# Two attention-and-mixture layers on one core: the second layer norm of sequence 0 placed beside the last block of the first attention, and the second layer's weights loaded into the first layer's tiles

## The chip, the cores and the metric

The kernel runs as one program on one core of a Trainium2 chip. The metric is the device time of that core in microseconds (us), the median of three executions. One more execution was recorded by the hardware profiler; all stretches of time below come from it.

## The reference, cut to what matters

The input is x with 2 sequences of 2048 tokens and 256 features, all float32. Two layers follow each other:

```python
xn = layernorm(x)
s  = attention0(xn)                 # 16 heads of 16 features, every token sees every token
g  = silu(ffn0(xn))                 # mixture of 16 low-rank branches, cumulative sums over the tokens
x  = x + s * g
xn = layernorm(x)
s  = attention1(xn)                 # 16 heads, a token sees only tokens at most 64 away
g  = silu(ffn1(xn))                 # dense base plus 8 low-rank experts with softmax gates
x  = x + s * g
```

`layernorm` takes mean and variance over the 256 features of each token, with eps 1e-5 and no scale or shift.

## The kernel before

**Layout.** Features lie on the 128 partitions (two chunks `c`), tokens along the free axis, in blocks of `TB` = 512 tokens (four blocks `n` for each sequence `b`). `x`, `xn` and `gt` stay in SBUF for both sequences. The program is traced once by a tile framework, which places waits and also decides each engine's order, from the order of the calls and its own estimates; what is wrapped in `keep_in_program_order` holds its place.

**Stages in order of time.** Weights and the first layer norm; the first ffn; the first attention (`attention(A0, ..., False, False)`, called at L840); the second layer norm with the gates (`layer_norms`, L95, called at L937, for eight blocks: both sequences); the second ffn (`experts`, L899); the second attention.

**First attention.** An item is one sequence, one group `g` of four heads and one block `n` of 512 queries: 32 items, 16 steps each, one step per 128 keys (`U` = 16). A step of the *second pass* of an item computes, for each of the four heads, the scores of 128 keys against the 512 queries on the PE (`sk`, L599, four concurrent row tiles of 32 rows), their exponentials on ScalarE (`e`, L615), and the weighted sum of the values on the PE (`acc`, L662, in `weigh`), which ScalarE copies out of PSUM (`av` or `more`, L669 and L672) and GpSimd adds up (L673). The *first pass* of an item, which finds the maximum of each query's scores, runs 19 steps ahead (`sq`, L599; its reduction on VectorE, L611). So in each step one item's first pass lies beside another item's second pass. In the last 19 steps (`LEAD` = 3 and the 16 of the last item) there is no first pass left. I number them s0-3 to s0+15, where s0 is the first step of the last item.

**PSUM in the first attention.** There are 8 banks of 128x512 float32. `pmax` (tag `sq`) has two tiles of two banks each; `pexp` (called `pm`, tag `m`) has four of one bank. While both passes run, the four `sk` and the `acc` of a step take five tiles from the four banks of `pm` in turn, and the two pairs of `sq` take `pmax`. In the last 19 steps the branch `not apart and j >= 2` (L559) puts two of the four `sk` into the idle `pmax` (`sk2`), so that a step takes only three tiles from `pm`.

**Order in a step.** `scores` issues the step's `sk` (and `sq`); then `weigh` issues the `acc` of the step before (`DEL` = 1); then come the calls that `at(step, f)` has put behind that step: the sums of an item are scattered by DMA, inverted and multiplied (`compact` to `divide`), and for the last group of heads two products with the output weights (`project`, L756: tile `pr`, then `upd` on VectorE, then an addition on GpSimd).

**Second layer norm.** For a block, `there` turns x on the PE so that tokens lie on the partitions (`xt`, L104, eight 128x128 transposes), takes mean and variance on VectorE (L108, L110), and forms two factors (`Sqrt` on ScalarE, L113, reciprocal and product on VectorE). `back` applies them on ScalarE (`xc`, L121), turns the result back (`xb`, L127, eight transposes) and copies it to `xn` (L129, one copy on each of ScalarE and VectorE). Between blocks the gates' logits of the block before are computed (`gates`, `tokens`); `normalized` is the softmax over experts and `turned` spreads the gates over partitions by way of DRAM.

**Weights.** `load_attn` loads the four matrices and four biases of an attention. The second layer's are loaded after the first attention is through (L845, on the SP queue), and the four tensors of its ffn on the ScalarE queue (L851 to L854).

## Time and profile before

| what | value |
|---|---|
| median of three executions | 2620.93 us (2620.79 to 2621.52) |
| the profiled execution | 2619.84 us, of which the span of the program 2618.1 us |
| granted TensorE clock, mean over the span | 0.991 |
| busy share of the span: PE, VectorE, ScalarE, GpSimd | 98%, 64%, 63%, 34% |

In the rows below PE is TensorE's matmuls and PEld its weight loads, DVE is VectorE, ACT ScalarE, POOL GpSimd, SP the queue of most DMAs. A row of the timeline gives the start, the time until its last instruction ends, the engine, the source line, what is written from what, and the count; in brackets stands the idle time before it and what ended that. The ends of matmuls are modelled, and consecutive instructions of one engine overlap, so the distance between starts is the better measure of a rate.

### The profile page before, as it was taken

What the parts mean: (1) busy time and instruction counts of PE and PEld (TensorE: products, weight loads), DVE (VectorE), ACT (ScalarE), POOL (GpSimd) and SP (SyncE); (2) the same over time, 40 slices, a digit from 0 to 9 for tenths busy, and PEclk for the clock granted to TensorE, in tenths of its full rate; (3) what the DMA queues carried; (4) which work ended last, traced back from release to release, by engine and by line L of the source; (5) the groups of instructions that cost most, each with busy time, mean ns of one, the idle gap of its engine ahead of it and who ended that gap; (6) DMA issues with size and microseconds to landing.
All of it is one profiled execution on the core that took longest, in us unless ns stands there. A gap on an engine that the chain in (4) does not pass through costs nothing.

```text
span 2618.1 us, 49275 instructions
## 1 busy us (share of the span) xinstructions
PE 2570.3 (98%) x19060; PEld 1099.6 (42%) x19060; DVE 1671.5 (64%) x2753; ACT 1641.1 (63%) x3200; POOL 894.9 (34%) x845
## 2 busy tenths in 40 slices
PE   8999999999999999999999999999999978999999
PEld 5444444543333333333333333333333324558776
DVE  4133332167888888888777888888888523228884
ACT  5300000228888888888778888888888854236655
POOL 0000000203444444444444444444444430206666
PEclk9999999999999999999999999999999989989999
DMA  4031110410001010010010010010000012411120
GB/s 150 3 88 45 53 45 32 99 64 4 8 12 19 8 24 9 6 25 8 6 25 8 6 25 8 6 27 6 8 8 6 10 30 35 96 67 39 46 58 35
DMA packets 58857, 82.08 MB, mean 31 GB/s; under 512 B 24160, under 2 KB 29152, under 8 KB 57040
## 3 DMA queue, kind: packets, MB, share of 16 engines
q1 hardware_dynamic: 56576, 77.36, 12.3%
q8 instruction: 150, 2.46, 0.4%
q10 hardware_dynamic: 2048, 1.58, 0.2%
q14 instruction: 83, 0.68, 0.1%
HBM read 52.22 MB, written 21.95 MB: 28 GB/s over the span
## 4 chain that ended last, share of the span: by engine, by line
PE 97%; DVE 1%; ACT 1%; DMA 0%; issue 0%; POOL 0%; SPq 0%; POOLq 0%; ACTq 0%; DVEq 0%
PE sk L599 25%; PE acc L662 22%; PE sq L599 19%; PE pp L446 4%; PE py L377 4%; PE po L357 4%; PE px L373 4%; PE ph L263 2%; PE pr L761 2%; PE pp L459 2%; PE psf L199 1%; PE po L909 1%; PE tr L687 1%; PE xb L127 1%; PE po L389 1%; PE xt L104 1%
## 5 line engine op out<-in xcount | busy, mean ns | idle before, releaser
L611 DVE TENSOR_REDUCE part<-sq 128x2 f32<-128x1024 f32 x1024 | 1206.7, 1220 | 304.2 <-PE sq L599 303.7
L615 ACT ACTIVATE e<-sk 128x512 f32<-128x512 f32 x2048 | 1062.7, 615 | 214.9 <-PE sq L599 192.2
L599 PE MATMUL sk<-q,k 32*128 32x512 f32 (+2 forms) x5632 | 1149.7, 533 | 0.6 <-ACT e L615 0.4
L599 PE MATMUL sq<-k,q 32*128 32x512 f32 (+2 forms) x5120 | 1140.8, 572 | 3.2 <-DVE part L611 1.7
L673 POOL TENSOR_TENSOR av<-av,more 128x512 f32<-128x512 f32 x480 | 607.7, 1266 | 961.2 <-ACT more L672 961.1
L599 PEld LDWEIGHTS sk<-q,k 32*128 32x128 f32 x5632 | 532.3, 184 | 581.1 <-ACT e L615 490.9
L662 PE MATMUL acc<-e,v 128*32 128x512 f32 x4096 | 550.6, 605 | 0.0
L599 PEld LDWEIGHTS sq<-k,q 32*128 32x128 f32 x5120 | 412.5, 184 | 28.0 <-DVE part L611 14.0
L672 ACT COPY more<-acc 128x512 f32<-128x512 f32 x480 | 287.8, 600 | 3.8 <-PE acc L662 1.7
L662 PEld LDWEIGHTS acc<-e,v 128*32 128x32 f32 x4096 | 82.4, 108 | 391.5 <-ACT e L615 387.0
L393 ACT ACTIVATE gt<-po 128x512 f32<-128x512 f32 x16 | 9.5, 596 | 324.6 <-PE po L389 324.6
L606 DVE CUSTOM_DVE_ANT_0 seen<-sq,mask 128x256 f32<-128x256 f32 (+1 forms) x512 | 177.4, 411 | 41.5 <-PE sq L599 32.8
L399 POOL TENSOR_TENSOR x<-x,up 128x512 f32<-128x512 f32 x16 | 20.2, 1264 | 416.4 <-DVE up L396 416.4
L620 POOL TENSOR_SCALAR_AFFINE_SELECT xn<-xn 128x512 f32<-128x512 f32 x172 | 103.1, 635 | 119.3 <-ACT xn L615 117.4
L381 DVE TENSOR_TENSOR xs<-we,px 128x512 f32<-128x512 f32 x64 | 43.8, 685 | 135.4 <-PE px L373 135.4
L373 PE MATMUL px<-xn,FV 128*128 128x512 f32 x256 | 121.2, 595 | 0.0
L377 PE MATMUL py<-cum,FW 128*128 128x512 f32 x256 | 120.5, 593 | 0.6 <-DVE cum L346 0.6
L615 ACT ACTIVATE xn<-sk 128x512 f32<-128x512 f32 x172 | 90.1, 601 | 48.2 <-PE sk L599 12.9
L357 PE MATMUL po<-pr,UO 128*128 128x512 f32 x256 | 119.0, 592 | 0.0
L383 DVE TENSOR_TENSOR pr<-xs,py 128x512 f32<-128x512 f32 x64 | 44.0, 687 | 62.4 <-PE py L377 62.2
L766 DVE TENSOR_TENSOR upd<-gt,pr 128x512 f32<-128x512 f32 x32 | 22.0, 687 | 86.0 <-PE pr L761 79.5
L357 PEld LDWEIGHTS po<-pr,UO 128*128 128x128 f32 x256 | 48.6, 190 | 61.2 <-issue 60.7
(169 smaller groups left out, 1683.2 us busy)
## 6 DMA issues: line engine op xcount, KB each, us to landing
we<-wd SPq DMA_DIRECT2D x128, 128.0 KB
qd<-sb SPq DMA_DIRECT2D x48, 256.0 KB
k<-qd SPq DMA_DIRECT2D x40, 128.0 KB
q<-qd SPq DMA_DIRECT2D x40, 128.0 KB
x<-in_x SPq DMA_DIRECT2D x8, 512.0 KB
q<-row SPq DMA_DIRECT2D x256, 2.0 KB
xn<-av SPq DMA_DIRECT2D x128, 32.0 KB
recb<-rd SPq DMA_DIRECT2D x128, 32.0 KB
```

What stands on the lines that cost most here:

```text
L357: nc.tensor.matmul(po[oc], UO[:, ch, bass.ts(oc, P)], pr, start=(ch == 0), stop=False)
L373: nc.tensor.matmul(px, FV[:, c, bass.ts(ch, P)], xn[b][:, c, cols], start=(c == 0), stop=(c == NC - 1))
L377: nc.tensor.matmul(py, FW[:, c, bass.ts(ch, P)], cum[:, c, :], start=(c == 0), stop=(c == NC - 1))
L446: nc.tensor.matmul(ps, w[:, c, bass.ts(hf, P)], xn[b][:, c, bass.ts(n, TB)], start=(c == 0), stop=(c == NC - 1))
L599: nc.tensor.matmul(o, lhs, rhs, start=True, stop=True)
L606: nc.vector.tensor_tensor_reduce(seen[:, lo:hi], sq[:, d, t * 2 * P + lo : t * 2 * P + hi], mask[:, lo:hi], 1.0, LOWEST, ALU.add, ALU.max, ...
L611: nc.vector.tensor_reduce(pt[:, pair[0] : pair[1] + 1, t, kb], sq, AX.X, ALU.max)
L615: nc.scalar.activation(e, t, AF.Exp, scale=scale)
L620: nc.gpsimd.affine_select(out=e[:, :, c, :], in_=e[:, :, c, :], compare_op=ALU.is_ge, fill=0.0, base=0, pattern=[[0, 4], [sign, P]], chann ...
L662: nc.tensor.matmul(acc[hp[j], o : o + hi - lo], vs[b][:, kt, vcols(g, j)], es[j][:, lo:hi], start=(r == 0), stop=(r == len(parts) - 1), sk ...
L672: nc.scalar.copy(more, acc)
L673: nc.gpsimd.tensor_tensor(avs[i], avs[i], more, ALU.add)
```

## The change

- `layer_norms` is split: `there`, `factors` and `back` can be used apart, and the second call handles only sequence 1 (four blocks).
- The four blocks of sequence 0 get their second layer norm within the last 16 steps of the first attention, two blocks at a time: `norm_there` behind s0 and s0+1 (and s0+8, s0+9), `norm_factors` for both blocks behind s0+2 (s0+10), `norm_back` behind s0+3 and s0+5 (s0+11, s0+13). `xt` takes the tiles of `pmax`, `xb` those of `pm`, `xc` those of the exponentials. VectorE, not ScalarE, applies the factors and makes both copies to `xn`.
- In the last 19 steps all four `sk` of a step come from `pm` (`tail`).
- The sums `av` and `more` of the last item are copied out of PSUM by VectorE instead of ScalarE.
- After the attention the gates and the softmax of sequence 0 come first, then the layer norms of sequence 1 with `turned` of sequence 0 and the gates of sequence 1 between them.
- The attention weights of both layers share tiles (`wat`). The second layer's q and k and the two low-rank factors of its ffn (in the tile of `wv`) are loaded at step 0 of the first attention, its o after it, its v after `experts`. Its biases, `gateT` and `baseT` are loaded with the first layer's weights.

```diff
-                        if not apart and j >= 2:
+                        if not apart and not tail and j >= 2:
...
+                copy = nc.vector.tensor_copy if not local and i == len(items) - 1 else nc.scalar.copy
...
                 elif u == 0:
-                    nc.scalar.copy(avs[i], acc)
+                    copy(avs[i], acc)
                 else:
                     more = op.tile([P, TB], F32, name="more", tag="more", bufs=2)
-                    nc.scalar.copy(more, acc)
+                    copy(more, acc)
...
+                def norm_there(n):
+                    if n % 2 == 0:
+                        norms["mv"] = op.tile([P, 2 * QT, 2], F32, name="mv", tag="mv")
+                    xt = norms[n] = pmax.tile([P, QT, D], F32, name="xt", tag="sq")
+                    st = op.tile([P, QT, 6], F32, name="st", tag="st")
+                    there(0, n, xt, norms["mv"][:, n % 2 * QT : (n % 2 + 1) * QT, :], st, pin)
+                def norm_factors():
+                    norms["f"] = op.tile([P, 2, 2 * QT], F32, name="nf", tag="nf")
+                    factors(norms["f"], norms["mv"], pin)
+                def norm_back(n):
+                    xt, f, xc = norms.pop(n), norms["f"], []
+                    for t in range(QT):
+                        if t % 2 == 0:
+                            xc.append(ep.tile([P, 2, D], F32, name="xc", tag="e"))
+                        r = n % 2 * QT + t
+                        nc.vector.tensor_scalar(
+                            xc[-1][:, t % 2, :], xt[:, t, :], f[:, 0, r : r + 1], f[:, 1, r : r + 1], ALU.mult, ALU.add
+                        )
+                    for c in range(NC):
+                        xb = pm.tile([P, TB], F32, name="xb", tag="m")
+                        for t in range(QT):
+                            nc.tensor.transpose(xb[:, bass.ts(t, P)], xc[t // 2][:, t % 2, bass.ts(c, P)], ident)
+                        nc.vector.tensor_copy(xn[0][:, c, bass.ts(n, TB)], xb)
+                for r in range(NB // 2):
+                    s0 = total - U + r * (U // 2)
+                    at(s0, norm_there, 2 * r)
+                    at(s0 + 1, norm_there, 2 * r + 1)
+                    at(s0 + 2, norm_factors)
+                    at(s0 + 3, norm_back, 2 * r)
+                    at(s0 + 5, norm_back, 2 * r + 1)
...
+    def second_weights():
+        pin = tc.keep_in_program_order
+        A1.update(q=weight(1, "q", pin), k=weight(1, "k", pin))
+        t = wat.tile([P, NC, D], F32, name="lUV", tag="wv")
...
-    attention(A0, 1.0 / float(np.sqrt(D)), False, False)
-    layer0.close()
+    attention(A0, 1.0 / float(np.sqrt(D)), False, False, second_weights)
...
-            blocks = [(b, n) for b in range(B) for n in range(NB)]
             held = {}
+            for n in range(NB + 1):
+                if n < NB:
+                    held[n] = gates(pg1, 0, n)
+                if n:
+                    tokens(pg1, *held.pop(n - 1))
+            normalized(0)
             def between(r):
+                if r == 1:
+                    turned(pg1, 0)
                 if r - 1 in held:
                     tokens(pg1, *held.pop(r - 1))
-                if 1 <= r <= len(blocks):
-                    held[r] = gates(pg1, *blocks[r - 1])
-                if r == NB + 1:
-                    normalized(0)
-                if r == NB + 3:
-                    turned(pg1, 0)
-            layer_norms(blocks, tb, pn1, between)
+                if r:
+                    held[r] = gates(pg1, 1, r - 1)
+            layer_norms([(1, n) for n in range(NB)], tb, pn1, between)
```

In the built program GpSimd's order is as before, and every other engine's order differs only from s0 to the end of the second layer norm, apart from where the weights' DMAs stand on their queues.

More of the change, by code (lines that the diff above doesn't have):

```diff
@@ L71, in rows, with weight, biases @@
         return ap.rearrange("(c p) m -> p c m", p=P)
-    def load_attn(pool, l, eng):
-        return dict(
-            q=load(pool, f"wq{l}", [P, NC, D], rows(a[f"wq{l}"]), eng),
-            k=load(pool, f"wk{l}", [P, NC, D], rows(a[f"wk{l}"]), eng),
-            v=load(pool, f"wv{l}", [P, NC, D], rows(a[f"wv{l}"]), eng),
-            o=load(pool, f"wo{l}", [P, NC, D], rows(a[f"wo{l}"]), eng),
-            bq=load(pool, f"bq{l}", [P, NC], a[f"bq{l}"], eng),
-            bk=load(pool, f"bk{l}", [P, NC], a[f"bk{l}"], eng),
-            bo=load(pool, f"bo{l}", [P, NC], a[f"bo{l}"], eng),
-            bv=load(pool, f"bv{l}", [P, NC], a[f"bv{l}"], eng),
-        )
+    wat = ctx.enter_context(tc.tile_pool(name="wat", bufs=1))
+    def weight(l, kind, issue=lambda i: i):
+        t = wat.tile([P, NC, D], F32, name=f"w{kind}{l}", tag=f"w{kind}")
+        issue(nc.sync.dma_start(out=t, in_=rows(a[f"w{kind}{l}"])))
+        return t
+    def biases(l):
+        return {b: load(wat, f"{b}{l}", [P, NC], a[f"{b}{l}"], nc.sync) for b in ("bq", "bk", "bo", "bv")}
     def whole_bias(A, ps):
@@ L93, in whole_bias, with there, factors, go @@
         nc.vector.tensor_tensor(A["bo"], A["bo"], ps[:, :NC], ALU.add)
+    QT = TB // P
+    def there(b, n, xt, mv, st, first=lambda i: i):
+        for t in range(QT):
+            for c in range(NC):
+                i = nc.tensor.transpose(xt[:, t, bass.ts(c, P)], x[b][:, c, bass.ds(n * TB + t * P, P)], ident)
+                if t + c == 0:
+                    first(i)
+        for t in range(QT):
+            nc.vector.bn_stats(st[:, t, :], xt[:, t, :])
+        for t in range(QT):
+            nc.vector.bn_aggr(mv[:, t, :], st[:, t, :])
+    def factors(f, mv, issue=lambda i: i):
+        issue(nc.scalar.activation(f[:, 0, :], mv[:, :, 1], AF.Sqrt, bias=eps_t))
+        nc.vector.reciprocal(f[:, 0, :], f[:, 0, :])
+        nc.vector.scalar_tensor_tensor(f[:, 1, :], mv[:, :, 0], -1.0, f[:, 0, :], ALU.mult, ALU.mult)
     def layer_norms(blocks, tmp, ps, between=lambda r: None):
-        QT = TB // P
-        def there(b, n):
+        def go(b, n):
             xt = ps.tile([P, QT, D], F32, name="xt", tag="xt")
-            for t in range(QT):
-                for c in range(NC):
-                    nc.tensor.transpose(xt[:, t, bass.ts(c, P)], x[b][:, c, bass.ds(n * TB + t * P, P)], ident)
             st = tmp.tile([P, QT, 6], F32, name="st", tag="st")
             mv = tmp.tile([P, QT, 2], F32, name="mv", tag="mv")
-            for t in range(QT):
-                nc.vector.bn_stats(st[:, t, :], xt[:, t, :])
-            for t in range(QT):
-                nc.vector.bn_aggr(mv[:, t, :], st[:, t, :])
+            there(b, n, xt, mv, st)
             f = tmp.tile([P, 2, QT], F32, name="f", tag="f")
-            nc.scalar.activation(f[:, 0, :], mv[:, :, 1], AF.Sqrt, bias=eps_t)
-            nc.vector.reciprocal(f[:, 0, :], f[:, 0, :])
-            nc.vector.scalar_tensor_tensor(f[:, 1, :], mv[:, :, 0], -1.0, f[:, 0, :], ALU.mult, ALU.mult)
+            factors(f, mv)
             return b, n, xt, f
@@ L132, in layer_norms @@
         for r in range(len(blocks) + 1):
-            first = there(*blocks[r]) if r < len(blocks) else None
+            first = go(*blocks[r]) if r < len(blocks) else None
             if held:
@@ L148, in softmax8 @@
         return rec
-    layer0 = ctx.enter_context(ExitStack())
-    wat0 = layer0.enter_context(tc.tile_pool(name="wat0", bufs=1))
     with tc.tile_pool(name="fw", bufs=1) as fw:
@@ L227, in two_layers @@
                 steps.pop(0)()
-        A0 = load_attn(wat0, 0, nc.sync)
+        gateT = wat.tile([P, NC, HP], F32, name="gateT")
+        nc.vector.memset(gateT, 0.0)
+        A0 = {**{k: weight(0, k) for k in "qkvo"}, **biases(0)}
         b1 = load(fw, "b1", [P, NC], a["r_b1"], nc.sync)
@@ L243, in two_layers @@
         nc.vector.reciprocal(rn, rn)
+        B1 = biases(1)
+        nc.sync.dma_start(out=gateT[:, :, :KE], in_=rows(a["gateT"]))
+        baseT = load(wat, "baseT", [P, NC, D], rows(a["weightT"]), nc.sync)
         ones = fw.tile([P, TB], F32, name="ones")
@@ L399, in two_layers, with attention @@
                             nc.gpsimd.tensor_tensor(x[b][:, oc, cols], x[b][:, oc, cols], up, ALU.add)
-    def attention(A, scale, local, final):
+    def attention(A, scale, local, final, start=None):
         items = [(b, g, n) for b in range(B) for g in range(NG) for n in range(NB)]
@@ L535, in scores @@
                 apart = second and first
+                tail = not local and not first
                 if second:
@@ L665, in weigh @@
                         )
+                copy = nc.vector.tensor_copy if not local and i == len(items) - 1 else nc.scalar.copy
                 if local:
-                    nc.scalar.copy(avs[i][:, bass.ts(u, 2 * P)], acc[:, : 2 * P])
+                    copy(avs[i][:, bass.ts(u, 2 * P)], acc[:, : 2 * P])
                 elif u == 0:
-                    nc.scalar.copy(avs[i], acc)
+                    copy(avs[i], acc)
                 else:
                     more = op.tile([P, TB], F32, name="more", tag="more", bufs=2)
-                    nc.scalar.copy(more, acc)
+                    copy(more, acc)
                     nc.gpsimd.tensor_tensor(avs[i], avs[i], more, ALU.add)
@@ L803, in attention @@
                     at(end, fetch, b * NG + g + 2, T // 2 if local else 0)
+            if start:
+                at(0, start)
+            if not local:
+                pin = tc.keep_in_program_order
+                norms = {}
+                def norm_there(n):
[9 more added lines that the diff above has]
+                    xt, f, xc = norms.pop(n), norms["f"], []
+                    for t in range(QT):
+                        if t % 2 == 0:
[4 more added lines that the diff above has]
+                        )
+                    for c in range(NC):
+                        xb = pm.tile([P, TB], F32, name="xb", tag="m")
+                        for t in range(QT):
+                            nc.tensor.transpose(xb[:, bass.ts(t, P)], xc[t // 2][:, t % 2, bass.ts(c, P)], ident)
[7 more added lines that the diff above has]
+                    at(s0 + 5, norm_back, 2 * r + 1)
             fetch(0)
@@ L838, in attention @@
                     f(*args)
-    attention(A0, 1.0 / float(np.sqrt(D)), False, False)
-    layer0.close()
-    wat1 = ctx.enter_context(tc.tile_pool(name="wat1", bufs=1))
-    A1 = load_attn(wat1, 1, nc.sync)
+    A1 = {}
+    lUV = []
+    def second_weights():
+        pin = tc.keep_in_program_order
+        A1.update(q=weight(1, "q", pin), k=weight(1, "k", pin))
+        t = wat.tile([P, NC, D], F32, name="lUV", tag="wv")
+        lUV.extend((t[:, 0, :].rearrange("p (c e) -> p c e", c=NC), t[:, 1, :]))
+        pin(nc.sync.dma_start(out=lUV[0], in_=rows(a["lUT"])))
+        pin(nc.sync.dma_start(out=lUV[1], in_=a["lVT"]))
+    attention(A0, 1.0 / float(np.sqrt(D)), False, False, second_weights)
+    A1.update(o=weight(1, "o"), **B1)
+    lU, lV = lUV
     with tc.tile_pool(name="gw", bufs=1) as gw, tc.tile_pool(name="tb", bufs=2) as tb, tc.tile_pool(
@@ L848, in two_layers @@
     ) as gdp:
-        gateT = gw.tile([P, NC, HP], F32, name="gateT")
-        nc.vector.memset(gateT, 0.0)
-        nc.scalar.dma_start(out=gateT[:, :, :KE], in_=rows(a["gateT"]))
-        baseT = load(gw, "baseT", [P, NC, D], rows(a["weightT"]), nc.scalar)
-        lU = load(gw, "lU", [P, NC, KE * R1], rows(a["lUT"]), nc.scalar)
-        lV = load(gw, "lV", [KE * R1, D], a["lVT"], nc.scalar)
         lg = gw.tile([P, B * NT, KE], F32, name="lg1")
@@ L923, in two_layers @@
         ) as pg1:
-            blocks = [(b, n) for b in range(B) for n in range(NB)]
             held = {}
+            for n in range(NB + 1):
[4 more added lines that the diff above has]
+            normalized(0)
             def between(r):
+                if r == 1:
+                    turned(pg1, 0)
                 if r - 1 in held:
                     tokens(pg1, *held.pop(r - 1))
-                if 1 <= r <= len(blocks):
-                    held[r] = gates(pg1, *blocks[r - 1])
-                if r == NB + 1:
-                    normalized(0)
-                if r == NB + 3:
-                    turned(pg1, 0)
-            layer_norms(blocks, tb, pn1, between)
+                if r:
+                    held[r] = gates(pg1, 1, r - 1)
+            layer_norms([(1, n) for n in range(NB)], tb, pn1, between)
             whole_bias(A1, pg1.tile([P, P], F32, name="pbias", tag="s"))
-            tokens(pg1, *held.pop(len(blocks)))
+            tokens(pg1, *held.pop(NB))
         with tc.tile_pool(name="pb", bufs=2, space=PSUM) as pb:
@@ L946, in two_layers @@
                         turned(pb, 1)
+    A1["v"] = weight(1, "v")
     attention(A1, float(HD ** -0.5), True, True)
```

## The prediction, written before the changed kernel ran

> **What bounds the kernel now.** I read the page, then busy time by stretch, then the timeline around the first attention's end, then groups by shape for durations.

> ```profile
> PE 2570.3 (98%) x19060; PEld 1099.6 (42%) x19060; DVE 1671.5 (64%) x2753; ACT 1641.1 (63%) x3200; POOL 894.9 (34%) x845
> ```

> A PE at 98% says little, since waiting between a matmul's start and modelled end counts too. Busy time in four stretches says more (columns PE, PEld, DVE, ACT, POOL, then granted PE clock, DMA share, GB/s): the 19 steps without a first pass, the end of the last sums, the second layer norm with the gates, the experts.

> ```profile
> 2069.40:2122.70 53.30, 53.30 (x334) 13.78 (x330) 4.28 (x9) 47.67 (x97) 30.29 (x24) 1.00 0.04 11
> 2122.70:2141.50 18.80, 5.68 (x8) 1.77 (x8) 1.63 (x3) 1.87 (x2) 5.03 (x6) 0.65 0.15 33
> 2141.50:2188.10 46.60, 36.51 (x289) 24.81 (x289) 25.26 (x112) 27.92 (x56) 1.26 (x1) 0.81 0.09 25
> 2188.10:2246.20 58.10, 57.14 (x145) 25.37 (x145) 17.88 (x29) 12.92 (x22) 0.58 (x1) 1.00 0.27 38
> ```

> In the first stretch VectorE is idle (4.28 of 53.30) and ScalarE nearly full; in the third no engine is, as PE, VectorE and ScalarE hand blocks to each other. The change moves half of the third into the first. What a step of each kind waits for shows in the timeline, first with both passes, then in the tail:

> ```profile
> 2063.72 0.58 ACT L672 COPY more<-acc 128x512 f32<-128x512 f32 x1
> 2064.68 2.06 ACT L615 ACTIVATE e<-sk 128x512 f32<-128x512 f32 x4 [0.38 <-PE sq L599]
> 2065.45 1.06 PE L662 MATMUL acc<-e,v 128*32 128x512 f32 x8
> 2066.45 0.70 PE L599 MATMUL sk<-q,k 32*128 32x512 f32 x2
> 2066.64 0.58 ACT L672 COPY more<-acc 128x512 f32<-128x512 f32 x1
> 2067.61 2.06 ACT L615 ACTIVATE e<-sk 128x512 f32<-128x512 f32 x4 [0.38 <-PE sq L599]
> ...
> 2102.10 1.45 PE L662 MATMUL acc<-e,v 128*32 128x512 f32 x8
> 2102.24 2.66 ACT L615 ACTIVATE e<-sk 128x512 f32<-128x512 f32 x4
> 2103.48 1.14 PE L599 MATMUL sk<-q,k 32*128 32x512 f32 x8
> 2104.16 1.22 ACT L672 COPY more<-acc 128x512 f32<-128x512 f32 x1
> 2104.55 1.45 PE L662 MATMUL acc<-e,v 128*32 128x512 f32 x8
> ```

> With both passes a step takes 2.93 (2064.68 to 2067.61), in the tail 2.45 (acc at 2102.10 and 2104.55). There ScalarE's queue is never empty: four exponentials and a copy start every 2.45.

> **Part 1: a tail step without norm work.** The copy leaves ScalarE, but all four `sk` now come from `pm`. Five tiles in turn from four banks: the built program's order makes `acc` wait for the first exponential of the step just issued (its bank), and the fourth `sk` for the copy of the last `acc`. That gives two loops. By the banks of `acc`: exponential 0.60, hand-over 0.05 (exponentials end 2104.90, the weight load that waits for them is at 2104.95), `acc` to next `sk` 1.00 (2065.45 to 2066.45), `sk` to exponential 1.16 (2066.45 to 2067.61): 2.81. By the bank of the fourth `sk`: `acc` 1.06, hand-over 0.13 (2063.59 to 2063.72), copy on VectorE 0.69 (row below), 0.05, `sk` to `acc` 1.07 (2103.48 to 2104.55): 3.00. The longer holds: 3.00 for 2.45. The 15 steps from the `acc` that starts at 2080.70 to that at 2118.71 took 38.0; they take 15 x 3.00 + 1.91 (one `project` product, as before) = 46.9, **+8.9**.

> The four steps before them (2068.38 to 2080.70, 12.3) get the same rotation with ScalarE's copy (0.58, so 2.89): 2.89, 3.1 with `place_max`, and twice a step with `project`, whose `upd` then holds the fourth `sk`'s bank: 1.00 + 1.98 + 0.10 + 0.69 + 0.05 + 1.07 = 4.89. Sum 15.8, **+3.5**.

> **Part 2: the norm work in the tail.** Its rows:

> ```profile
> 2172.36 1.04 PE L104 MATMUL xt<-ident,x 128*128 128x128 f32 x8
> 2143.60 1.42 DVE L108 BATCH_NORM_STATS2 st<-xt 128x6 f32<-128x256 f32 x4 [2.18 <-PE xt L104]
> 2166.11 1.28 ACT L144 ACT_TABLE_LOAD   x1
> 2167.41 0.31 ACT L144 ACTIVATE lg<-lg 128x128 f32<-128x128 f32 x1
> L129 DVE COPY xn<-xb 128x512 f32<-128x512 f32 x16 | 11.0, 689 | 15.3 <-ACT xn L129 15.3
> ```

> `norm_there`: eight transposes, 1.04, stand on the PE between `acc` and `sk`, in the 2.81 loop: 3.85 for 3.00; four times, **+3.4**. Statistics (1.42) and aggregates (0.36) lie on idle VectorE, ahead of the next copy, and end 3.9 after that step's `acc` starts; the next `acc` ends at 4.9, so they are hidden. Were steps 1 us shorter, they would show.

> `norm_factors`: `Sqrt` stands in ScalarE's queue between exponentials and needs another table. Exponentials end 2.05 after the first starts, load 1.30, `Sqrt` 0.31, load 1.30: the next can start after 4.96, and all of the PE's next work waits for it. 4.96 for 3.00, twice: **+3.9**. [...] In the row the next instruction starts 0.02 after the load; the sum goes by the row.

> `norm_back`: put `acc`'s start at 0. VectorE's first `xc` needs a buffer that this `acc` frees (1.1); the copy of `acc` stands behind it (to 2.2), then three more `xc` (0.36 apart, as the statistics, which read the same shape) to 3.2. The PE puts two transposes ahead of `sk`, then two `sk` (the second waits for the copy, so the PE is held to 3.2), then six transposes (to 4.0), and `sk` three and four, whose banks wait for new exponentials (4.25); `acc` follows 1.07 later at 5.3. Then a plain 3.00: 8.3 for two steps instead of 6.0; four times, **+9.2**. Bounds: transposes alone, 4 x 1.04 = 4.2, if the waits overlap; 4 x 5 = 20, if each wait adds in full. I take the order's sum.

> The last sums' chain (18.8) keeps its links: VectorE's copy is 0.1 longer than ScalarE's, **+0.1**.

> Tail: 8.9 + 3.5 + 3.4 + 3.9 + 9.2 + 0.1 = **+29.0**.

> **Part 3: what leaves the layer norm's stretch.** Before, from the first `xt` to the first product of the experts it took 46.6, the first `xn` copy 9.2 after its start. Now gates of sequence 0 come first: two blocks of logits, their transpose and two more, about 6.4 with the first transposes of `x` between; softmax, seven small VectorE steps of 0.17 to 0.29 with statistics between and one exponential, 3.3: 9.7. Four turnings of 1.0 at half clock, taken in turn with ScalarE's copies and the `Sqrt`, then `xc`, `xb`: first `xn` copy at 15.7. Three more blocks at 3.8 (before, copies at 2150.68 to 2161.98), then the last gates, 2.2: 29.3. So **-17.3**; by the slowest spacing seen among those blocks (4.4) -15.5, by the quickest (3.4) with the softmax hidden under the transposes -21.

> **Part 4: weights.** The four early loads stand behind the q and k stores and ahead of a scatter of maxima 13 steps later; what they wait for (the last values product) is done one step earlier. The six added loads at the start stand behind everything on SP that the first ffn needs. The load of the second v waits for the last `experts` product and has until 2273.9 (27.7 of q and k products), against at most a few us for 256 KB. Before, the second layer's loads were hidden too. Nothing, bounds -1 to +1. The experts' stretch is PE work (57.14 of 58.10): no change.

> **Sum.** 29.0 - 17.3 = +11.7. The profiled execution, 2619.84 (span 2618.1, 1.7 around it), becomes 2631.5; the median is 1.1 above it, so 2620.93 + 11.7, about **2632**.

> **Rivals.** *Faster*: ScalarE paces the tail, the banks give way in time, and with the copies gone a step falls to the PE's own 1.07 + 1.00 = 2.07. For it: ScalarE's queue never empties in the tail. Against it: the waits of the built order. Then -5.7 for 15 steps, +4.2 and +4.2 for transposes, +3 for half-hidden table loads: tail +5.7, with -17.3 about 2609. It decides as soon as the tail adds less than 12 in all. *Same*: the exponential's loop (2.81) holds, not the copy's, and `norm_back` costs its transposes: 5.4 + 3.0 + 3.4 + 3.9 + 4.2 - 17.3 = +2.6, 2623.5. *Slower still*: the PE's clock. In the rows above it is 0.65 and 0.81 where the PE has gaps and 1.00 in the tail, and eight transposes took 1.91 in place of 1.04 when it was half. The new tail has gaps of some 2.5 at the table loads and in `norm_back`; if the six steps concerned do 2 us of PE work each at half clock, +12: 2644. [...]

> **How the numbers follow.** A measurement here tells 0.2% (5.2 us) from no change. The main case has 0.58 and the clock's 0.12, both slower: 0.70; the same case 0.15, the faster 0.15. The range starts at 2618 (the same case less 3.7 for the quick layer norm and 1 for the weights) and so leaves out the faster case; it ends at 2643, short of the clock's 2644.

> **What would show it.** Right: between 2069 and the last `acc`, 19 steps take some 82 in place of 53; plain steps 3.0, ended by VectorE's copy; 5.0 at the `Sqrt`; GpSimd and VectorE busy throughout; from there to the experts 48 in place of 65. Wrong: plain steps at 2.1 to 2.5, or `norm_back` pairs near 7, or a layer norm stretch far from 29.

## The result: slower by 28 us, and the profile after

The changed kernel takes 2649.05 us (median of four: 2644.15, 2645.01, 2653.09, 2657.66), the kernel before beside it 2620.86: a ratio of 1.0112, 95% interval 1.0094 to 1.0129. The forecast was 2632, range 2618 to 2643. The direction was right, the size was not.

The profiled execution is the longest of the four (2657.66, span 2655.9, so +37.8 on the span before). This is the page's line of engines:

```profile
PE 2602.4 (98%) x19060; PEld 1111.3 (42%) x19060; DVE 1692.7 (64%) x2785; ACT 1627.1 (61%) x3164; POOL 895.9 (34%) x845
```

Like the line before the change, it says little, and the stretches say more. Busy time in the same four stretches as in the prediction, bounded by the same events: tail, end of the last sums, layer norm with gates, experts (columns PE, PEld, DVE, ACT, POOL, granted PE clock, DMA share, GB/s):

```profile
2071.44:2174.51 103.07, 93.75 (x398) 30.43 (x394) 34.41 (x83) 48.10 (x88) 30.46 (x25) 0.74 0.01 4
2174.51:2193.15 18.64, 5.33 (x8) 1.76 (x8) 2.32 (x4) 0.00 (x0) 4.88 (x4) 0.73 0.08 18
2193.15:2222.82 29.67, 23.60 (x224) 15.26 (x224) 14.99 (x68) 15.48 (x31) 1.28 (x1) 0.81 0.26 46
2222.82:2284.01 61.19, 60.23 (x145) 26.41 (x145) 17.99 (x29) 13.02 (x22) 0.58 (x1) 0.95 0.13 18
```

The tail grew from 53.3 to 103.1 and its granted clock fell from 1.00 to 0.74. The layer norm fell from 46.6 to 29.7. The experts took 3.1 more, at a clock of 0.95. The whole program stood 2.0 later before the tail began. 2.0 + 49.8 - 0.2 - 16.9 + 3.1 = 37.8, all of it.

The forecast tail was 82, so some 21 us in the tail are not in the forecast's steps. The next fence shows where they start: the PE's timeline from the first table switch to the end of the first `norm_back` step and the plain step behind it.

```profile
2093.65 1.07 PE L677 MATMUL acc<-e,v 128*32 128x512 f32 x8 [0.67 <-ACT e L630]
2094.65 2.07 PE L614 MATMUL sk<-q,k 32*128 32x512 f32 x8
2098.64 1.67 PE L677 MATMUL acc<-e,v 128*32 128x512 f32 x8 [1.92 <-ACT e L630]
2100.99 0.66 PE L850 MATMUL xb<-ident,xc 128*128 128x128 f32 x2 [0.69 <-DVE xc L844]
2101.58 2.08 PE L614 MATMUL sk<-q,k 32*128 32x512 f32 x4
2103.59 1.54 PE L850 MATMUL xb<-ident,xc 128*128 128x128 f32 x6
2105.06 2.08 PE L614 MATMUL sk<-q,k 32*128 32x512 f32 x4
2107.07 1.94 PE L677 MATMUL acc<-e,v 128*32 128x512 f32 x8
2108.93 3.02 PE L614 MATMUL sk<-q,k 32*128 32x512 f32 x8
2111.89 1.94 PE L677 MATMUL acc<-e,v 128*32 128x512 f32 x8
```

From `acc` to `acc` the switch step takes 2098.64 - 2093.65 = 4.99 (forecast 4.96), and the PE idles 1.92 in it. From then on the same eight records of `acc` take 1.94 in place of 1.07. The `norm_back` step takes 8.43 and the plain one 4.82: 13.25 where the forecast had 8.3. In windows of 3.41 us, the grid on which the clock changes in the trace (its stretches at half clock last 30.72, 23.89, 13.65, 10.24 and 3.41, all multiples of 3.41):

```profile
2092.17:2095.59 3.42, 2.75 (x21) 0.75 (x14) 2.18 (x9) 2.57 (x5) 0.00 (x0) 1.00 0.11 22
2095.59:2099.00 3.41, 1.49 (x10) 0.45 (x10) 0.37 (x2) 3.37 (x6) 1.26 (x1) 1.00 0.00 0
2099.00:2102.41 3.41, 2.72 (x12) 0.79 (x6) 2.11 (x5) 1.06 (x3) 0.82 (x1) 0.50 0.00 0
2102.41:2105.83 3.42, 3.42 (x12) 1.65 (x10) 1.69 (x3) 1.09 (x2) 0.44 (x1) 0.50 0.00 0
...
2126.31:2129.72 3.41, 3.41 (x16) 1.00 (x8) 0.69 (x1) 0.72 (x2) 1.26 (x1) 0.50 0.00 0
2129.72:2133.13 3.41, 3.41 (x25) 1.33 (x24) 1.64 (x4) 1.75 (x4) 1.04 (x1) 1.00 0.00 0
```

### The profile page after: what moved, and what is told of

The parts are those of the page before. It is cut to its first block, busy times and chain, and to the rows that moved or that the text cites. A ratio compares the mean times of both kernels' runs of the same rounds, so it can differ in the third digit from the quotient of the medians.

```text
span 2655.9 us, 49280 instructions
## 1 busy us (share of the span) xinstructions
PE 2602.4 (98%) x19060; PEld 1111.3 (42%) x19060; DVE 1692.7 (64%) x2785; ACT 1627.1 (61%) x3164; POOL 895.9 (34%) x845
## 4 chain that ended last, share of the span: by engine, by line
PE 97%; DVE 1%; ACT 1%; DMA 0%; issue 0%; POOL 0%; SPq 0%; POOLq 0%; ACTq 0%; DVEq 0%
PE sk L614 26%; PE acc L677 22%; PE sq L614 18%; PE pp L460 4%; PE py L389 4%; PE po L369 4%; PE px L385 4%; PE pr L778 2%; PE ph L275 2%; PE pp L473 2%; PE psf L206 1%; PE po L970 1%; PE tr L704 1%; PE pt L964 1%; PE po L401 1%; PE po L974 1%
## 5 line engine op out<-in xcount | busy, mean ns | idle before, releaser
L614 PE MATMUL sk<-q,k 32*128 32x512 f32 (+2 forms) x5632 | 1175.1, 539 | 0.6 <-ACT e L630 0.4
L614 PEld LDWEIGHTS sk<-q,k 32*128 32x128 f32 x5632 | 542.3, 186 | 584.4 <-ACT e L630 484.2
L614 PEld LDWEIGHTS sq<-k,q 32*128 32x128 f32 x5120 | 413.2, 184 | 27.7 <-DVE part L626 14.0
L689 ACT COPY more<-acc 128x512 f32<-128x512 f32 x465 | 272.3, 586 | 2.2 <-issue 1.3
L635 POOL TENSOR_SCALAR_AFFINE_SELECT xn<-xn 128x512 f32<-128x512 f32 x172 | 103.0, 634 | 119.3 <-ACT xn L630 117.4
L389 PEld LDWEIGHTS py<-cum,FW 128*128 128x128 f32 x256 | 48.5, 190 | 61.4 <-issue 59.7
```

Source lines behind the costliest of these rows:

```text
L389: nc.tensor.matmul(py, FW[:, c, bass.ts(ch, P)], cum[:, c, :], start=(c == 0), stop=(c == NC - 1))
L614: nc.tensor.matmul(o, lhs, rhs, start=True, stop=True)
L635: nc.gpsimd.affine_select(out=e[:, :, c, :], in_=e[:, :, c, :], compare_op=ALU.is_ge, fill=0.0, base=0, pattern=[[0, 4], [sign, P]], chann ...
L689: copy(more, acc)
```

## Experiments

**Theory A (clock):** the step model of the prediction is right, and the excess is half clock, started by the PE's idle time at the table switch. **Theory B (hand-overs):** the `norm_back` steps take 13 us a pair by their own waits, and the low clock is only their sign. The first two experiments set them apart; all times are medians, with ratios to the kernel before on the same chip. Lists of step lengths are intervals between the starts of successive `acc` in the trace.

**No table switch.** `norm_factors` leaves ScalarE alone, and with it the square root:

```diff
-                    norms["f"] = op.tile([P, 2, 2 * QT], F32, name="nf", tag="nf")
-                    factors(norms["f"], norms["mv"], pin)
+                    f = norms["f"] = op.tile([P, 2, 2 * QT], F32, name="nf", tag="nf")
+                    mv = norms["mv"]
+                    nc.vector.tensor_scalar(f[:, 0, :], mv[:, :, 1], EPS, None, ALU.add)
+                    nc.vector.reciprocal(f[:, 0, :], f[:, 0, :])
+                    nc.vector.scalar_tensor_tensor(f[:, 1, :], mv[:, :, 0], -1.0, f[:, 0, :], ALU.mult, ALU.mult)
```

> The changed kernel without the two square roots in the tail: norm_factors takes the reciprocal of the variance plus eps on VectorE and leaves the root out, so no activation table is switched between the exponentials. Theory A (clock): the profile of after shows a 3.41 us window 44% busy at each table switch, then half clock for 30.7 and 23.9 us; without the switches these steps take 3.0 in place of 5.0, no window is that empty, and the norm_back pairs take 8.3 in place of 13.3: tail (first tail acc to last acc) 78 in place of 103, about 2628 (2625 to 2633). Theory B (hand-overs): the norm_back steps take 8.4 and 4.8 by their own waits and the low clock is only a sign of them: 2 x 2.0 us less than after, about 2645 (2642 to 2648). Between the two (2634 to 2641): norm_back's own gaps lower the clock without a table switch, later than before.

Measured: 2629.61, ratio 1.0040 (1.0027 to 1.0052); the tail took 78.4 from its first to its last `acc`, with no half clock in it. The steps from the first `norm_there` on are 3.83, 3.83, 3.00, 5.46, 3.00, 5.46, 3.00, 3.00 and so on. Theory A within 2 us, and B is out: `norm_back` with all its hand-overs takes 8.46 a pair at full clock. Its gaps alone lowered nothing here.

**The switch kept, the gap filled.** More work, same values computed:

```diff
                 for _, o, lhs, rhs in sorted(pieces, key=lambda x_: x_[0]):
                     nc.tensor.matmul(o, lhs, rhs, start=True, stop=True)
+                if tail and second and i == len(items) - 1 and u in (3, 11):
+                    for _, o, lhs, rhs in 2 * pieces[2:]:
+                        nc.tensor.matmul(o, lhs, rhs, start=True, stop=True)
```

> The changed kernel with more work: in the two steps whose exponentials stand behind the table switch, the products of the third and fourth head's scores are issued twice more (same data into the same bank), some 2 us of PE work in the PE's idle 1.9 us. Theory A (clock): the window is no longer empty, the clock stays whole, the switch step still takes 5.0, the norm_back pairs 8.3 in place of 13.3: about 2632 (2629 to 2637), faster than after although it does more. Theory B (hand-overs): the pairs stay above 12 and the time is that of after or a little more, 2647 to 2653. If products of two heads count too little for the clock, as B.

Measured: 2634.71, ratio 1.0062 (1.0050 to 1.0075): eight products more, 14 us less than the changed kernel. Its tail, and the window of the first switch on the grid of 3.41 us:

```profile
2069.97:2152.47 82.50, 76.56 (x414) 27.78 (x410) 34.30 (x83) 48.13 (x88) 30.55 (x25) 1.00 0.02 4
2095.17:2098.58 3.41, 2.86 (x17) 0.69 (x13) 0.69 (x3) 3.38 (x6) 0.25 (x1) 1.00 0.00 0
```

The clock is 1.00 in the whole tail, and the window is busy for 2.86 in place of 1.49. Its timeline at the switch and in the first `norm_back` step:

```profile
2093.62 1.28 ACT L112 ACT_TABLE_LOAD   x1
2094.91 0.30 ACT L112 ACTIVATE nf<-mv,eps_t 128x8 f32<-128x8 f32 x1
2095.04 1.93 PE L617 MATMUL sk<-q,k 32*128 32x512 f32 x7
2095.23 1.28 ACT L633 ACT_TABLE_LOAD   x1
2096.53 2.06 ACT L633 ACTIVATE e<-sk 128x512 f32<-128x512 f32 x4
2097.18 1.06 PE L680 MATMUL acc<-e,v 128*32 128x512 f32 x8 [0.21 <-ACT e L633]
...
2102.63 1.06 PE L680 MATMUL acc<-e,v 128*32 128x512 f32 x8
```

The extra products (L617) run while ScalarE changes tables; `acc` takes 1.06 after it, and the `norm_back` step 2102.63 - 2097.18 = 5.45. Nothing was taken off ScalarE, so the switch costs 2.0 by itself (5.00 from the `acc` at 2092.18 to that at 2097.18, for 3.00 in a plain step), as forecast, and the other 14 us were the clock.

**No norm at all, and then the gaps alone.** Both kernels leave out the norm of sequence 0 (the loop of its five `at` calls is deleted), so the second layer works on the old `xn` there. The second one puts two table switches on constant numbers back:

```diff
+            if not local:
+                def switch():
+                    mv = op.tile([P, 2 * QT, 2], F32, name="mv", tag="mv")
+                    nc.vector.memset(mv, 1.0)
+                    f = op.tile([P, 2, 2 * QT], F32, name="nf", tag="nf")
+                    factors(f, mv, pin)
+                at(total - U + 2, switch)
+                at(total - U + 10, switch)
```

> The changed kernel without the norm of sequence 0 (left out altogether, so its second layer works on the old xn): the tail keeps the VectorE copies and the four sk from the four banks that acc shares. The plain step, which after showed only at half clock (4.82), is 3.00 by the prediction's loop: tail 53.2 + 8.9 + 3.5 = 65.6 and 17 less in the layer norm: about 2616 (2613 to 2619), clock whole in the tail. Theory A and B agree on it. If the banks give way (the rival called faster), plain steps are 2.07 to 2.45 and the time 2602 to 2607.

> The changed kernel without the norm of sequence 0 (left out, as in the third experiment) but with the two square roots on constant numbers, so the two table switches alone stand in a tail of plain steps; the experiment without them had 2619.6. Theory A without help from norm_back: each switch costs its own 2.0 and empties one window, the clock halves, and as the plain step at half clock took 4.82 in after with bank waits in it, it stays half until the project steps or the next full window: +10 to +25, 2630 to 2645. If norm_back's hand-overs are what holds the clock low, plain steps bring it back in one or two windows: 2626 to 2630. If a gap alone does not lower the clock, 2 x 2.0 and no more: 2623 to 2625.

Measured without the norm: 2619.55, ratio 0.9998 (0.9989 to 1.0007). Every plain step of the last item takes 3.00, as the loop of banks said; the tail is 65.1 (forecast 65.6). The total is 3.5 above the forecast and just outside its range, because in its profile the layer norm took 31.5 and the experts 1.7 more than before.

```profile
2102.19 0.69 DVE L689 COPY more<-acc 128x512 f32<-128x512 f32 x1 [2.31 <-PE acc L677]
...
2103.98 1.06 PE L677 MATMUL acc<-e,v 128*32 128x512 f32 x8
2104.98 2.07 PE L614 MATMUL sk<-q,k 32*128 32x512 f32 x8
2105.18 0.69 DVE L689 COPY more<-acc 128x512 f32<-128x512 f32 x1 [2.15 <-PE acc L677]
```

`sk` takes 2.07 for its eight records, where with its own banks it took 1.14: the fourth waits for the copy (2105.18 to 2105.87) while ScalarE and the PE wait for it.

Measured with the two switches: 2624.72 (2624.03 to 2631.36), ratio 1.0018 (1.0010 to 1.0027), 5.2 more. By the time alone this would be the case in which a gap lowers nothing (2623 to 2625). The profile shows otherwise. The windows of the first switch:

```profile
2091.92:2095.33 3.41, 1.61 (x10) 0.45 (x10) 0.61 (x4) 3.37 (x5) 1.26 (x1) 1.00 0.01 1
2095.33:2098.75 3.42, 3.42 (x16) 1.01 (x8) 0.69 (x1) 1.14 (x3) 1.02 (x1) 0.50 0.00 0
2098.75:2102.16 3.41, 3.23 (x21) 1.04 (x16) 0.69 (x1) 2.60 (x6) 0.90 (x2) 1.00 0.00 0
```

The gap alone lowered the clock, in the profiled execution for one window (3.41 us) each time, and plain steps brought it back. That plain steps would leave it low is refuted. Four of the eleven executions took 2626.80 to 2631.36, at a mean granted clock of 0.988 to 0.989, so half clock may have lasted longer there. So the switches cost 5.2, the norm without switches 10.1 (2629.61 - 2619.55), the sum over 2619.55 is 2634.8; the filled kernel has 2634.7, the changed one 14 more. That is an interaction: the gap lowered the clock, and with `norm_back` following at once it stayed low, for 30.7 and 23.9 us in the profile of after.

**The same work, with two plain steps between.**

```diff
-                    s0 = total - U + r * (U // 2)
+                    s0 = total - U - 1 + r * (U // 2)
...
-                    at(s0 + 3, norm_back, 2 * r)
-                    at(s0 + 5, norm_back, 2 * r + 1)
+                    at(s0 + 5, norm_back, 2 * r)
+                    at(s0 + 7, norm_back, 2 * r + 1)
```

> The changed kernel with the same work in another order: the norm starts one step earlier and each norm_back comes two steps later after its norm_factors, so that two plain steps stand between the table switch and the next norm_back. Without the norm the two switches cost 5.2 us (half clock for one window each, ended by plain steps); without the switches the norm cost 10.0 us and the clock stayed whole; the sum, from the kernel without the norm at 2619.6, is 2634.8, and after has 2649. If it takes both together (the gap lowers the clock, norm_back's steps at half clock keep it low), the clock is back before norm_back begins and the time is that sum, 2632 to 2638. If a switch and a norm_back in one tail suffice at any distance, half clock lasts again and the time stays at 2643 to 2655.

Measured: 2638.00 (2635.58 to 2646.78), ratio 1.0073 (1.0060 to 1.0086). Half clock lasts 6.8 and 3.4 us after the two switches in its profile, in place of 30.7 and 23.9, and all four `norm_back` steps that follow run at full clock (5.46 each for the three that stand clear of other work). The median lies at the upper end of the forecast, and one execution in five still has 2646.8. The order alone gives back about 10 of the 14 us.

**What keeps the clock low.** An extra product of two heads in the plain step after the first `norm_back` of each pair (the edit of the filled kernel with `u in (5, 13)` and once in place of twice), and the changed kernel again:

> The changed kernel with its table switches as they are, and one extra product of two heads' scores (same data, same bank) in the plain step after the first norm_back of each pair, where the clock is already half. What holds the clock low for 30.7 and 23.9 us although the PE is never idle for more than 0.6 us at a stretch? Theory H1: half clock lasts until one whole window is full, and the bank waits of some 0.8 us in each half-clock step prevent that; the extra work fills one window and the clock returns a step later: some 10 us less than after, 2634 to 2642. Theory H2: the clock returns by itself after a time, or by the transposes; the extra work only adds: 2647 to 2655.

> The changed kernel itself once more, beside the one before on the same chip, since its four times lie in two pairs (2644.2 and 2645.0; 2653.1 and 2657.7) and the product added after the first norm_back of each pair gave 2643.5 to 2652.9. If the extra work shortens the half clock, the changed kernel has a median of 2648 to 2653 and mostly the upper values; if the length of the half clock depends on how the 3.41 us windows fall on the steps, its times lie between 2643 and 2658 in the same two groups and the extra work did nothing.

Measured: 2644.51 (2643.49 to 2652.88), ratio 1.0100 (1.0084 to 1.0115); the changed kernel again 2647.48 (2644.60 to 2656.14), ratio 1.0114 (1.0098 to 1.0131). The two overlap. In the profile with the extra product half clock lasts 27.3 and 10.2 us, in that of the changed kernel again 10.2 and 23.9: stretches as short come without it. So these times do not part H1 from H2. The traces do say something on H1, though: at half clock the PE idles up to 0.7 us at a stretch (0.71 ahead of the `xb` at 2114.53 in the profile of after), not 0.6, and by the trace's busy time whole windows were full without the clock coming back, from 2102.41 on in the profile above. H1 can hold only if the busy time shown counts waiting that the clock does not count, and no run shows that. It does show that the changed kernel's times vary with how long the two stretches last (10.2 to 30.7 us seen); that the phase of the 3.41 us grid against the steps decides this is plausible and was not shown.

**The copies alone.** The kernel before with one line of the change, the `copy` that is VectorE's for the last item; the spare banks stay.

> The kernel before with one part of the change alone: the last item's sums are copied by VectorE instead of ScalarE; the two spare banks of the scores stay. If ScalarE's queue paced the tail (four exponentials and a copy in 2.45), a step falls to the PE's own 2.07 or the exponentials' 2.06: 15 x 0.38 = 5.7 less, 2615 (2614 to 2617). If a bank paces it, the copy's bank comes free 0.1 later and the step stays at 2.45 to 2.6: 2620 to 2623.

Measured: 2616.78, ratio 0.9987 (0.9978 to 0.9996). Steps alternate between 2.07 and 2.24 in place of 2.45; the tail is 49.7 for 53.2. So ScalarE's queue did pace the tail of before, and the copies are worth 3.5 there (3.2 in the medians on the same chip) as long as the scores keep their own banks. With the shared banks (65.1) that is lost four times over.

**The weights alone.** The kernel before with only the new places of the weights.

> The kernel before with the weights' part of the change alone: one pool for both layers' weights, gate, base and bias loads at the start, four early loads inside the first attention, second o and v late; no copy and no norm moved. The prediction's term is 0 (bounds -1 to +1): 2619 to 2622. If the six loads at the start hold up the first ffn, or the late load of the second v the second attention, 2623 or more. The start of after stood 2.0 us later than in before, those of the first two experiments' profiles 0.3 us earlier and 0.6 later, so a shift there is expected to come and go between executions of one kernel.

Measured: 2620.43, ratio 0.9997 (0.9988 to 1.0006). In its profile the layer norm took 2.1 less and the experts 1.7 more, which nearly cancel. Nothing, as forecast.

**Another place.** The first attention ends with a chain of DMAs in which the PE idles for 13 of 19 us (18.80, of which 5.68 busy). This kernel leaves the scores their spare banks and issues the norm there, block by block, with `xc` on ScalarE and one table load. Of its edit the places are shown:

```diff
-                tail = not local and not first
+                tail = False
...
+                at(total + 1, norm_go, 0)
+                at(total + 1, norm_go, 1)
+                at(total + 6, norm_back, 0)
+                at(total + 6, norm_go, 2)
+                at(total + 7, norm_back, 1)
+                at(total + 15, norm_go, 3)
+                at(total + 15, norm_back, 2)
+                at(total + 16, norm_back, 3)
```

(`norm_go` is the transposes, statistics and factors of one block; `norm_back` centres, turns back and copies.)

> Another place for the moved work: VectorE copies and weights as in the change, but the scores keep their two spare banks, and the norm of sequence 0 is issued after the last product of the attention, beside the chain of DMAs that divides the last sums (PE idle 12 us of 20), with one table load, xc on ScalarE and copies by turns. Tail as with the copies alone, 49.7 (-3.5); the chain 20 to 22 (+1), layer norm to the experts 29 (-17), experts as in the other variants +1.7: about 2602 (2598 to 2607), clock no matter, as the PE's idle stretch is filled rather than made. If the norm's VectorE work delays the division, the chain takes 25 and more: 2606 to 2612.

Measured: 2602.56 (2600.52 to 2602.79), ratio 0.9926 (0.9913 to 0.9938): faster than both kernels. Its tail, chain and layer norm:

```profile
2069.97:2119.77 49.80, 49.80 (x334) 13.02 (x331) 14.45 (x23) 42.91 (x83) 30.67 (x25) 1.00 0.04 7
2119.77:2138.76 18.99, 14.13 (x74) 9.66 (x75) 12.37 (x48) 11.63 (x25) 5.64 (x5) 0.91 0.11 29
2138.76:2166.83 28.07, 21.02 (x225) 14.52 (x225) 14.90 (x68) 16.27 (x32) 0.52 (x1) 0.88 0.29 41
```

The chain takes 19.0 as in the kernels without the norm in it (18.8 and 18.6), with the PE busy for 14.1 of it in place of 5.7: the moved work is free there. The clock in it is 0.91, in place of 0.65. The tail is that of the copies alone (49.7), and the layer norm stretch is 28.1 in place of 46.6.

## Why the prediction was wrong

**Part 1, the plain and the early steps: right.** 3.00 forecast, 3.00 measured without the norm. The four early steps have 2.88, 3.01, 4.81 and 4.88 for 2.89, 3.1, 4.89 and 4.89. The waits decoded from the built order, each priced from a row, gave the step to 0.1 us.

**Part 2, the norm's steps at full clock: right.** `norm_there` 3.83 for 3.85, `norm_factors` 4.99 for 4.96, a pair with `norm_back` 8.46 for 8.3. The filled kernel's tail is 29.2 longer than before (82.5 for 53.3); the sum said 29.0. Loads, root and exponentials follow each other within 0.02 in the filled kernel's rows (load at 2093.62 for 1.28, root at 2094.91, load at 2095.23 for 1.28, exponentials at 2096.53), as the row of the prediction had it.

**The clock: this step failed.** It stood in the text as the rival "slower still", with a chance of 0.12 and a price of 12, and the forecast was made without it. There are two mistakes in it. One is the condition. I had written that gaps of some 2.5 at the table loads could halve the clock, and left it out of the forecast all the same; the low chance was my estimate, with no row of before behind it. An idle stretch of 1.92 in a window with 1.49 of PE work was enough, and 1.61 of PE work in the experiment with the gaps alone, while windows with 2.75 stayed at full clock. The profile of before held the warning in its layer norm, in windows that the prediction does not show. Three of these are the last at full clock before a drop:

```profile
2145.47:2148.88 3.41, 0.69 (x3) 0.31 (x3) 2.05 (x12) 2.02 (x6) 0.00 (x0) 1.00 0.03 4
2148.88:2152.29 3.41, 3.41 (x20) 2.42 (x21) 0.69 (x1) 2.79 (x6) 0.00 (x0) 0.50 0.00 0
...
2162.53:2165.95 3.42, 2.53 (x23) 1.07 (x22) 3.10 (x14) 2.20 (x7) 0.00 (x0) 1.00 0.00 0
2165.95:2169.36 3.41, 3.39 (x21) 2.84 (x21) 0.75 (x4) 3.38 (x7) 0.00 (x0) 0.50 0.00 0
2169.36:2172.77 3.41, 1.97 (x27) 1.60 (x22) 3.04 (x15) 1.04 (x3) 0.00 (x0) 1.00 0.00 0
2172.77:2176.19 3.42, 1.89 (x25) 0.98 (x23) 2.69 (x12) 3.17 (x7) 0.00 (x0) 1.00 0.00 0
2176.19:2179.60 3.41, 2.73 (x17) 1.60 (x18) 1.27 (x5) 2.74 (x7) 0.00 (x0) 0.50 0.02 5
```

The window from 2172.77, with 1.89 of PE work and idle stretches of up to 1.1, stands ahead of a drop. A tail step of 4.96 with PE work of 1.07 and 1.14 in it is emptier than that. But the busy time of a window does not decide alone: the window from 2169.36 kept the clock with 1.97, and that from 2162.53 lost it with 2.53. In the tails of all the profiles it does part the cases: each of the ten windows with 1.2 to 1.7 of PE work was followed by half clock, and none with 2.4 or more. So the warning made a drop likely, not certain, and no rule for it comes out of these runs.

The other mistake is the price. I took six steps with 2 us of PE work each. In the profile half clock lasted 54.6 us in the tail, through plain steps too, which took 4.82 in place of 3.00: 103.0 against 82.4, so 20.6 in the profiled execution and 14 in the medians. Plain steps brought the clock back within one window or two (3.4 us after both switches of the gaps alone, 6.8 and 3.4 in the kernel with the other order), while with `norm_back` behind the switch it took three to nine (10.2 to 30.7 us).

**Part 3: right.** 29.7 for 29.3, so -16.9 for -17.3; the profiles of the variants that keep this part have 28.1 to 31.5. **Part 4: right for the weights, wrong for "the experts: no change".** From their first product to their last the experts take some 1.7 more in most variants (58.5 for 56.8), and 3.1 in the profile of after. In each of these profiles half clock falls into their first microseconds; in before and in the copies alone, where they take 56.8, it does not. So it goes with whether half clock reaches into them. That the new places of the loads have no part in it is not shown: the kernel with these alone has the 1.7, too. That 256 KB take at most a few us shows in the profile of before: the second layer's four matrices of that size are issued from 2140.30 to 2141.77, and the DMAs move 335 GB/s from 2142 to 2144, 156 to 2146 and 4 to 2148.

**The other rivals.** *Faster* was wrong on the banks: they do not give way. Its premise, that ScalarE paces the tail of before, was right and brought 3.5 once the banks were left alone. *Same* was wrong: the copy's loop holds, not the exponential's. (Its 5.4 for the 15 steps would be 6.1 by the way Part 1 counts: 15 x 2.81 + 1.91 - 38.0.)

Summed with what was measured: tail +29.2, layer norm -16.9, experts +1.7 and the clock in the tail +14 make +28.0; measured were 28.2. The 14 is itself the difference of two kernels' times, the changed and the filled one; what the sum tests is the other 14.0, against 14.7 for the filled kernel beside the kernel before on its chip (2634.71 - 2620.01).

## What to carry to other kernels

When a change puts a stall of 1 or 2 us on the PE in a stretch that ran at full clock, look at the trace's windows of 3.41 us: how full would the window with the stall be, and what follows it? Price the steps behind it at half clock too, down to the first dense stretch, and take that as the likely case where the window gets half empty; here it came each time in the tail (ten windows with 1.2 to 1.7 of PE work), though not each time elsewhere (1.97 kept the clock in the layer norm of before). If the stall can't be avoided, fill it with products that do no harm (14 us here), or put dense steps behind it (about 10); better, move work into time in which the PE idles anyway rather than into a stretch that is full (2602.56 here, for 2620.91).

## What was not expected of the hardware

- Eight extra products made the kernel 14 us faster (2634.7 for 2649.05), by keeping one window in each half of the tail busy (the first 2.86 of 3.41 in place of 1.49).
- After a gap in plain steps half clock lasted one window or two (3.4 and 6.8 us), and with `norm_back` behind the gap three to nine (10.2 to 30.7 us), with the PE shown busy for 2.7 us or more of each 3.41. What in `norm_back` keeps it low (its products of two heads at a time, its short waits, or its transposes) is open; the one experiment on it did not settle it.
- One program's executions lay between 2644 and 2658, with more half clock in the longer ones (mean granted clock 0.987 in the two shorter, 0.981 and 0.982 in the two longer), a spread of 13.5 us. The kernels without these gaps spread less, but not all of them little: 1.9 us without the square roots, 2.3 with the norm in the other place, 4.7 without the norm, 8.0 with the copies alone.
